# Lending a finished matrix's columns twice as load buffers, and moving mask conversions to earlier column groups

## The chip, the cores and the metric

The kernel runs on one core of a Trainium2 chip. The metric is device time in microseconds, the median of several runs.

## The reference

Two graph layers over N = 4096 nodes with D = 512 features, cut to what matters:

```python
x = layernorm(x + relu(adj @ (step(x) @ sign(w0).T)))        # layer 0
node_att = softmax(x @ node_w, axis=0)                       # layer 1
h = x @ edge_w                                               # <- the stage of this change
e = where(adj > 0, h @ h.T, -9e15)
edge_att = softmax(e, axis=1)
out = adj * (node_att * edge_att) @ (x @ weight) + bias
x = layernorm(x + out)
```

`adj` is 4096 x 4096 in f32, symmetric in where it is not zero, and mostly zero.

## The kernel before, in words

It has three stages, and the middle one is short.

1. Layer 0 (up to 505 us). For each block of 128 rows `adj` is multiplied with the weights. The result is normalised and transposed into `x1T` (feature-major, 4 x 128 features by 4096 nodes).
2. The product with edge_w, `h = x @ edge_w`, kept transposed in `hT` (the same shape: 4 row blocks k = 0 to 3, and 8 columns of 512 nodes, c = 0 to 7). It is what the change touches.
3. `h @ h.T` in blocks, the softmax, and the last product with `adj`.

**The masks.** Stage 3 wants for each pair of nodes a mask that is 0 where there is an edge and a large negative number where there is none. The mask is made ahead of time. A piece of `adj` (128 x 1024, f32, 512 KB) is loaded (`load_mask`, line 411). VectorE turns it, in place, into bf16 (`mask`, line 398, "conversion" from here on). The result (256 KB) is stored to `mask_d` in DRAM (`store`, line 401), and the buffer goes back to the list `bufs`. There are 80 pieces: 54 are made during stage 1, and the last 26 during stage 2.

**Buffers for these 26.** There are four proper ones, named `more`. Eight further ones are parts of `hT` itself: the columns 2, 6, 3 and 7, two row blocks at a time, are empty until the product reaches them. These are the "lent columns". Before the change each of the eight is used once (list `once`): after its store it isn't returned. The other 14 pieces go round on the four `more` buffers.

**The order of stage 2.** The product runs in four column groups g = 0 to 3 ("first" to "fourth"). Group g makes the columns g and g + 4 of `hT`. Each group is one call of `seven`, a scheme that gets a 2 x 2 block product from seven smaller ones (matmuls at line 99); in the second to fourth group three of the seven are split again in the same manner (line 116). The sums are gathered in PSUM banks. ScalarE (ACT) copies from them at lines 163 and 182, and VectorE (DVE) adds from them at lines 184, 191, 172, 166 and 169; a bank can be filled anew once the addition that reads it is done. All three engines work in the order in which the code was written (`manual_schedule`), so an instruction that waits holds up everything behind it on its engine. Lines 137 and 140 are small additions within the split products, line 605 prepares operands on VectorE, and lines 562 to 565 do so on GpSimd (POOL).

**Where the conversions stand.** `seven` calls `between_h` every few matmuls, 48 times in all (`count[0]` = 0 to 47, so twelve per group). At counts chosen by a condition, `between_h` makes one conversion. Three counts later it has ACT issue that piece's store. Then it has SP issue the next load into any buffer that has come free. The loads go through SP's queue and the stores through ACT's, each in order. A load into a used buffer waits for the store that reads it.

**What counts as a conflict.** The layer that places the waits compares, for two accesses to one tile, the stretches from first to last element. Row blocks of `hT` lie one after another, 4096 elements each.

## Time and profile before

| What | Value |
|---|---|
| Median of 3 runs | 1903.18 us (1902.19 to 1904.84) |
| The profiled execution's own time | 1902.74 us |
| Its span in the profile | 1901.0 us |
| Granted TensorE clock | 1.00 in every part of stage 2 |
| Stage 2, first matmul at line 99 to the first at line 885 | 505.31 to 601.29 us |
| Conversions on `more` buffers and in `hT` columns | 18 and 8 |

Busy time by stretch of stage 2 (us within the stretch; the share is that of the 16 DMA engines):

| Stretch, us | PE | DVE | ACT | POOL | DMA share | GB/s |
|---|---|---|---|---|---|---|
| 528 to 552 (second group) | 23.86 | 23.20 | 7.26 | 14.51 | 0.46 | 158 |
| 552 to 575 (third group) | 23.00 | 17.79 | 7.26 | 10.46 | 0.51 | 166 |
| 575 to 601.3 (fourth group) | 24.78 | 18.68 | 8.96 | 1.09 | 0.69 | 226 |

How to read it: PE is TensorE. Its matmuls overlap, and their ends are modelled, so a busy PE isn't one at its best pace; the distance between the starts tells the pace. A note in brackets behind a row of the timeline is the idle time of that engine just before, with the work whose end released it. A row with "x8" is eight instructions of one kind merged.

### The profile page before, as it was taken

The page shows a single profiled execution, that of the slowest core. Times are in us where ns is not written, and L with a number is a line of the kernel's source. Part 1 is how long each engine was busy: PE and PEld are TensorE (multiplying, and loading weights), DVE is VectorE, ACT ScalarE, POOL GpSimd, SP SyncE. Part 2 cuts the span into 40 slices and gives each one's busy share as a digit, 9 for nine tenths or more (in the row PEclk, how much of TensorE's full clock was granted, in tenths as well). Part 3 has the DMA queues.
Part 4 walks back from the last instruction along what each step waited for, and adds up shares of the span by engine and source line. Part 5 has one row for each costly group of instructions (what it writes and reads, how often), then busy time and mean ns, then how long its engine had stood idle before and what let it go on. Part 6 is the DMA issues. An engine that isn't in the chain of part 4 may idle for free.

```text
span 1901.0 us, 21535 instructions
## 1 busy us (share of the span) xinstructions
PE 1888.1 (99%) x7108; PEld 1273.2 (67%) x7108; DVE 1541.7 (81%) x2439; ACT 1039.4 (55%) x1714; POOL 334.9 (18%) x471
## 2 busy tenths in 40 slices
PE   9999999999999999999999999999999999999998
PEld 6888888888655656565567556666666666656646
DVE  7777677777888789788896888898879988898947
ACT  6433333333232567676677667665676567667732
POOL 0133132233550111111120111111111101110100
PEclk9999999999999999999999999999999999999999
DMA  9889898898747478577794978888877877787731
GB/s 324 295 324 359 310 338 322 329 354 291 276 163 262 145 266 341 190 267 274 282 342 165 320 282 294 288 288 297 276 279 285 295 269 281 266 315 251 286 116 56
DMA packets 149936, 521.01 MB, mean 274 GB/s; under 512 B 15040, under 2 KB 21696, under 8 KB 142144
## 3 DMA queue, kind: packets, MB, share of 16 engines
q1 hardware_dynamic: 65392, 235.43, 36.5%
q0 software_dynamic: 65552, 241.72, 33.3%
q10 hardware_dynamic: 18880, 42.47, 6.1%
q8 instruction: 56, 0.92, 0.2%
q14 instruction: 56, 0.46, 0.1%
HBM read 397.93 MB, written 121.63 MB: 273 GB/s over the span
## 4 chain that ended last, share of the span: by engine, by line
PE 87%; DVE 7%; DMA 3%; ACT 2%; issue 1%; SPq 0%; DVEq 0%; ACTq 0%
PE bank L1553 33%; PE acc L525 11%; PE acc L524 11%; PE bank L1151 11%; PE po L1703 4%; PE pt L847 3%; PE bank L946 2%; PE bank L885 2%; PE bank L1110 2%; PE bank L1073 2%; PE seven L99 2%; DVE lent L1322 1%; PE pt L484 1%; DVE slot L1322 1%; PE acc L306 1%
## 5 line engine op out<-in xcount | busy, mean ns | idle before, releaser
L1553 PE MATMUL bank<-lent,lop 128*128 128x256 f32 (+1 forms) x1368 | 433.2, 467 | 1.3 <-DVE lent L1334 0.6
L524 PE MATMUL acc<-xw,hi 128*128 128x512 f32 x960 | 376.5, 392 | 0.0
L525 PE MATMUL acc<-xw,lo 128*128 128x512 f32 x960 | 374.2, 390 | 0.0
L1553 PEld LDWEIGHTS bank<-lent,lop 128*128 128x128 f32 x1368 | 259.2, 190 | 146.7 <-issue 119.6
L1553 PE MATMUL bank<-slot,lop 128*128 128x512 f32 (+1 forms) x928 | 335.5, 508 | 0.7 <-DMA lop<-lop_d 0.5
L1553 PEld LDWEIGHTS bank<-slot,lop 128*128 128x128 f32 x928 | 176.0, 190 | 137.2 <-issue 122.8
L514 ACT CAST hi<-at 128x1024 fp32r<-128x1024 f32 x120 | 126.5, 1054 | 203.2 <-PE acc L524 152.9
L1564 ACT COPY over<-bank 128x512 f32<-128x512 f32 x200 | 116.0, 585 | 195.6 <-PE bank L1553 192.0
L525 PEld LDWEIGHTS acc<-xw,lo 128*128 128x128 f32 x960 | 180.3, 188 | 37.1 <-DVE lo L516 0.3
L524 PEld LDWEIGHTS acc<-xw,hi 128*128 128x128 f32 x960 | 180.3, 188 | 36.8
L516 DVE TENSOR_TENSOR lo<-at,hi 128x1024 fp32r<-128x1024 f32 x120 | 148.9, 1241 | 63.6 <-ACT hi L514 63.2
L818 ACT ACTIVATE line<-line,nmax_c 128x512 f32<-128x512 f32 x160 | 115.4, 727 | 20.9 <-DVE nmax_c L809 20.4
L1715 DVE SCALAR_TENSOR_TENSOR xb<-po,f,xb 128x256 f32<-128x256 f32 x84 | 40.3, 481 | 75.0 <-PE po L1703 74.9
L809 DVE CUSTOM_DVE_ANT_0 line<-lent,slot 128x512 f32<-128x512 bf16 x144 | 93.2, 691 | 8.9 <-ACT slot L848 6.1
L1526 ACT COPY bank<-over 128x512 f32<-128x512 f32 x144 | 86.8, 603 | 0.0
L847 PEld LDWEIGHTS pt<-ident,lent 128*128 128x128 f32 x406 | 50.9, 141 | 36.6 <-issue 23.8
L885 PE MATMUL bank<-hT 128*128 128x512 f32 (+3 forms) x256 | 75.1, 433 | 0.0
L1322 DVE CUSTOM_DVE_ANT_1 lent<-lent,line 128x2048 f32<-128x2048 f32 x32 | 73.0, 2284 | 2.4 <-DMA lent<-s_d 2.4
L485 ACT COPY x1T<-pt 128x512 f32<-128x512 f32 x32 | 18.8, 587 | 101.7 <-PE pt L484 101.7
L848 ACT COPY slot<-pt 128x512 f32<-128x512 f32 (+3 forms) x125 | 68.1, 554 | 11.5 <-PE pt L847 11.5
L1322 DVE CUSTOM_DVE_ANT_1 slot<-slot,line 128x2048 f32<-128x2048 f32 x32 | 73.1, 2284 | 0.0
L1328 ACT ACTIVATE slot<-slot 128x2048 f32<-128x2048 f32 x35 | 67.3, 1924 | 10.2 <-DMA slot<-in_adj_t_dram 10.2
(414 smaller groups left out, 3353.6 us busy)
## 6 DMA issues: line engine op xcount, KB each, us to landing
lop<-lop_d SPq DMA_DIRECT2D x154, 512.0 KB, 4.4
at<-in_adj_t_dram SPq DMA_DIRECT2D x60, 1024.0 KB, 6.9
slot<-in_adj_t_dram POOLq DMA_DIRECT2D x37, 1024.0 KB, 8.0
s_d<-slot POOLq DMA_DIRECT2D x32, 1024.0 KB, 8.1
slot<-s_d POOLq DMA_DIRECT2D x31, 1024.0 KB, 7.4
lent<-s_d POOLq DMA_DIRECT2D x29, 1024.0 KB, 8.0
lent<-in_adj_t_dram POOLq DMA_DIRECT2D x27, 1024.0 KB, 7.8
lent<-in_adj_dram SPq DMA_DIRECT2D x48, 512.0 KB, 6.3
```

The source lines that it names most:

```text
L514: nc.scalar.copy(hi, aq)
L516: nc.vector.tensor_sub(lo, aq, hi.bitcast(F32))
L524: nc.tensor.matmul(acc, hi[:, c, :], xw[:, kb, :], start=(kb == 0), stop=False)
L525: nc.tensor.matmul(acc, lo[:, c, :], xw[:, kb, :], start=False, stop=(kb == NB - 1))
L809: nc.vector.tensor_tensor_reduce(line, mask, src, -1.0, HUGE, ALU.add, ALU.min, accum_out=nmax_c[:, b, c : c + 1])
L818: nc.scalar.activation(line, line, AF.Exp, bias=nmax_c[:, b, c : c + 1], scale=-1.0, accum_out=sum_c[:, b, c : c + 1])
L847: nc.tensor.transpose(pt[:, j, :], src[:, ts(j, P)], ident)
L885: nc.tensor.matmul(pe[:, lo * P :], hT[:, k, ts(A * BG + i, P)], hT[:, k, (B * BG + lo) * P : (B + 1) * W], start=(k == 0), stop=(k == KD ...
L1151: nc.tensor.matmul(ps, left[m][:, k, q, :], right[m][:, k, :], start=(first and k == 0), stop=(k == KD // 2 - 1), skip_group_check=not first,)
L1322: pinned[0](nc.vector._custom_dve(TENSOR_ADD_SAT, out=q, in0=q, in1=m, s0=0.0, s1=-HUGE))
L1553: nc.tensor.matmul(ps, lop[:, k, :], rop[:, k, :], start=start, stop=(k == K - 1), skip_group_check=True)
L1564: nc.scalar.copy(self.to(), self.bank[:, : self.w])
```

## The change

Two things are changed. The lent columns 3 and 7 form a list of their own, `twice`. After its first store such a buffer goes back to `bufs`, so it is loaded a second time, and it is added to `once`, so that the second store is its last. The columns 2 and 6 stay in `once`. In the first round the order of loading is now `more`, columns 3 and 7, columns 2 and 6. Then 10 pieces instead of 14 go round on the `more` buffers.

The condition for the conversions becomes a list of 26 counts. By group (twelve counts each) the conversions were 3, 8, 8 and 7; with the list they are 3, 9, 9 and 5.

```diff
-        once = []
+        once, twice = [], []
...
                 def store():
                     queue.dma_start(mask_d[r][:, c : c + 2, j, :], m)
-                    if not any(a is b for b in once):
-                        bufs.append(a)
+                    for list_ in (once, twice):
+                        if any(a is b for b in list_):
+                            once.append(a)
+                            if list_ is once:
+                                return
+                            break
+                    bufs.append(a)
...
-        once.extend(hT[:, k : k + 2, ts(c, W)] for c in (2, 6, 3, 7) for k in (0, HK))
+        twice, once = ([hT[:, k : k + 2, ts(c, W)] for c in (n, n + HG) for k in (0, HK)] for n in (3, 2))
         bufs.extend(m[:, n, :].rearrange("p (c w) -> p c w", c=2) for m in more for n in range(2))
+        bufs.extend(twice)
         bufs.extend(once)
...
-            if count[0] in (4, 5, 7, 12) or count[0] > 12 and count[0] % 3 and count[0] not in (20,):
+            if count[0] in [4, 5, 7, 12, 13, 14, 16, 17, 18, 19, 21, 22, 24, 25, 26, 28, 29, 30, 32, 33, 34, 36, 37, 39, 41, 42]:
                 if loaded:
                     made.append((count[0], mask(nc.scalar)))
```

Line numbers in the text are those of the kernel before; from line 403 on the changed kernel's lie five or six higher.

## The prediction

> **What bounds the kernel now.** I read the page's first part, then the matmul timeline of the stage that the diff touches, then who keeps it waiting.

> ```profile
> span 1901.0 us, 21535 instructions
> PE 1888.1 (99%) x7108; PEld 1273.2 (67%) x7108; DVE 1541.7 (81%) x2439; ACT 1039.4 (55%) x1714; POOL 334.9 (18%) x471
> ```

> TensorE is the bound throughout; another engine costs time only where it makes TensorE wait. The product with edge_w (lines 99 and 116) runs from 505.31 to 601.29 us, 95.98 us. Its fourth column group ends so (start, duration, instruction, idle before):

> ```profile
> 588.93 3.60 PE L99 MATMUL seven<-x1T,lops 128*128 128x512 f32 x8
> 592.99 3.70 PE L99 MATMUL seven<-t,lops 128*128 128x512 f32 x8 [0.46 <-DVE hT L191]
> 597.75 3.70 PE L99 MATMUL seven<-t,we_s 128*128 128x512 f32 x8 [1.06 <-DVE hT L166]
> 601.29 4.89 PE L885 MATMUL bank<-hT 128*128 128x512 f32 x12
> ```

> Eight such matmuls take 3.43 us from start to start when nothing holds them (569.57 to 573.00 in the third group). Here the three steps take 4.06, 4.76 and 3.54, so 0.63 + 1.33 + 0.11 = 2.07 us are lost. The "idle" at the line's end is less, because the modelled ends overlap. VectorE's timeline says why:

> ```profile
> 588.38 0.69 DVE L398 TENSOR_SCALAR more<-more 128x1024 bf16<-128x1024 f32 x1 [2.63 <-DMA more<-in_adj_dram]
> ...
> 591.65 0.69 DVE L398 TENSOR_SCALAR more<-more 128x1024 bf16<-128x1024 f32 x1
> 592.25 1.28 DVE L191 TENSOR_TENSOR hT<-hT,seven 128x512 f32<-128x512 f32 x2
> 593.45 0.69 DVE L172 TENSOR_TENSOR hT<-hT,seven 128x512 f32<-128x512 f32 x1
> 595.21 0.69 DVE L398 TENSOR_SCALAR more<-more 128x1024 bf16<-128x1024 f32 x1 [1.07 <-DMA more<-in_adj_dram]
> ```

> A mask conversion (L398) waits for its load, and the additions that empty the PSUM banks (L191, L172, L166) queue behind it. The conversions come round on four `more` buffers: store, reload and conversion do not fit between two uses. The second group has a smaller loss of the same kind:

> ```profile
> 542.77 0.69 DVE L398 TENSOR_SCALAR hT<-hT 128x1024 bf16<-128x1024 f32 x1
> ...
> 545.17 0.69 DVE L398 TENSOR_SCALAR hT<-hT 128x1024 bf16<-128x1024 f32 x1
> ...
> 545.89 0.69 DVE L191 TENSOR_TENSOR hT<-hT,seven 128x512 f32<-128x512 f32 x1
> ...
> 546.63 3.70 PE L99 MATMUL seven<-t,lops 128*128 128x512 f32 x8
> ...
> 546.83 0.69 DVE L191 TENSOR_TENSOR hT<-hT,seven 128x512 f32<-128x512 f32 x1 [0.25 <-DMA mask_d<-hT]
> ```

> TensorE starts at 546.63 where 542.89 + 3.43 = 546.32 was possible: it waited for L191, so VectorE has no slack here. The last row is the key one. That L191 writes columns 1 and 5 of hT, yet it waits for the store of a lent buffer in columns 2 or 6. The recorded dependencies cover the whole stretch between a buffer's first and last element: two rows k, k+1 of column c reach over every later column of row k and every earlier one of row k+1. Any two lent buffers with the same two rows thus count as overlapping.

> [...]

> ```profile
> more<-in_adj_dram SPq DMA_DIRECT2D x16, 512.0 KB, 4.8
> mask_d<-more ACTq DMA_DIRECT2D x18, 256.0 KB, 3.5
> hT<-in_adj_dram SPq DMA_DIRECT2D x8, 512.0 KB, 7.7
> mask_d<-hT ACTq DMA_DIRECT2D x8, 256.0 KB, 2.3
> ```

> These are medians, issue to landing, over 500 to 610 us; the shortest load of this line is 3.7 and the shortest store 2.1 us. I go by the trace. [...]

> **The change, part by part.** Number the 26 conversions of this stage 1 to 26. It adds and removes none: 26 conversions at 0.60 us, 26 loads and 26 stores remain, as does every matmul. It moves them: before, 3, 8, 8 and 7 conversions stand in the four groups, after it 3, 9, 9 and 5.

> *Fourth group.* Two conversions fewer, and the last ones take loads issued earlier. Conversion 25 needs the reload that follows the store of conversion 21 (about 576 us): 576 + 2.1 + 4.8 = 583 us, against 585.8 when VectorE comes to it. Conversion 26 likewise: store about 580.8, landing about 588, VectorE there at about 588.3. L191 then starts behind L140 at about 589.6 instead of 592.25, with TensorE needing it only at 592.36. Nothing in the middle holds L166. Gain 2.07 us, say 2.0; if reload 26 takes the 6.7 us of the longest single one here, L137 is 2 us late and still in time.

> *Second group.* Conversions 5 to 8 use the columns 3 and 7 ("twice"), 9 to 12 the columns 2 and 6 ("once"). Positions up to conversion 8 (542.77 to 543.46) are the old ones. Now SP issues four reloads R5 to R8 into columns 3 and 7 right behind the stores of 5 to 8. By the overlap rule R5 also waits for conversion 7, R6 for 8, R7 for 9 and R8 for 10; in turn conversion 9 waits for R5, 10 for R6, 11 for R7 and 12 for R8, though none of these reads that data. Conversions 10, 11 and 12 stand directly ahead of L191, L166 and the second L166.
> - Conversion 9 (new before L137): 0.60 us, and R5 (issued 539.2, landing 543 to 544) hardly holds it.
> - Conversion 10: R6 can't be issued before 543.5. With the shortest landing, 3.7, conversion 10 starts at 547.2, L191 at 547.85 and ends at 548.5, and TensorE starts about 2.0 us later than now. With 4.4 it is 2.6 us, with 4.8 about 3.1, with 6.7 about 5. I take 4.4: the DMA share from 538 to 544 is only 0.33, but from 544 to 550 it is 0.70, with GpSimd's lop_d writes at 542.69 and 543.67. Cost 2.6, bounds 2.0 and 5.
> - Conversion 11: ACT copies L163 first (behind conversion 9, so 544.7 to 545.3), then issues store 7: landing 547.7. R7 lands 4.4 later, 552.1. L166 ends at 552.15 + 0.6 + 0.7 = 553.4; TensorE wants it at 549.25 + 3.43 = 552.7. Cost 0.7, bounds 0 and 2.
> - Conversion 12: store 8 also waits for R6 (they share a semaphore count): 548 + 2.4 + 4.4 = 554.8, so the second L166 ends at 556.2. TensorE, with a half product and four quarters between, wants it at 553.4 + 1.72 + 1.72 = 556.8. Hidden by 0.6 us. On ACT's queue store 10 waits for R8, and the copies L120 queue behind it (about 556 instead of 552.5); TensorE wants them some 4 us into the next group, 557.5. Hidden too, barely.

> SP's queue carries nothing else here: the next stage's loads (from 601.59) wait for the last matmul that reads x1T. Sum for the second group 3.3 us.

> *Third group.* All loads but the late ones are in. Conversion 18 fills an idle 0.94 us that VectorE has at 564.2. One new wait: the first L166 must wait for the store of conversion 18, which ACT issues behind that of 17, which waits for L172 (569.7): 570.2 + 2.1 = 572.3, L166 ends at 573.0, just when TensorE wants it (573.00). With the store at 3.1 it is 1 us late. Cost 0.5, bounds 0 and 2.

> *Afterwards.* The next stage starts behind the last matmul, and TensorE is busy 10.00 of 10 us from 605 to 615; a shift passes on one to one. Sum: 2.6 + 0.7 + 0.5 - 2.0 = +1.8; the bounds of the wait terms lie further above than below, so I take +2.2. The profiled execution took 1902.74 us (span 1901.0); 1902.74 + 2.2 = 1904.9. The median of the runs is 0.44 above it: 1905.4.

> **The rivals.**
> - *New waits outweigh the gain* (forecast): net +0.5 to +3.8, 1905.4; chance 0.50. For it: the chain of L398, reload, L398 is in the built program, and R6 can't be issued earlier.
> - *The waits bite less* (the other side): faster. It decides from the point where R6 lands before VectorE comes to conversion 10 at about 546.0, 2.5 us after issue. Then only conversion 9's 0.60 us is added: 0.6 + 0 + 0.3 - 2.0 = -1.1, 1902.1. Against it: no load here took under 3.7 us. For it: false waits cost only 0.25 us so far, and VectorE might be ahead of the old trace. With the cases that cancel, -2 to +0.5: chance 0.23, of it 0.03 faster by over 0.2%.
> - *The waits pile up*: reloads and stores share the DMA engines and each store waits for a reload, so R6 takes the 7.7 us of the first loads into hT, R7 and R8 follow late, and TensorE waits again at the head of the third group: 6 + 1.5 + 1.5 - 2.0 = +7, 1910; from +3.8 up, chance 0.27. Against it: those eight were queued together at a DMA share of 0.93.

> **How the numbers follow.** 0.2% is 3.8 us, about what a measurement of this kernel can tell from no change. Faster by more 0.03; slower by more 0.27; the rest 0.70. The range leaves out about 0.1 on each side: from 1901.9 (net -1.3) to 1908.9 (net +5.7).

> **What would show it.** In the fourth group L398 with no wait for a load, and steps of 3.43 us up to L885. In the second group, an L398 on hT that waits for a load into hT for 1 to 2 us, directly ahead of L191, and TensorE's step after 542.89 at about 6 us instead of 3.74; a second, smaller one ahead of L166. In the third, L166 waiting for a store of hT. It is wrong if the second group keeps its 23.53 us (528.36 to 551.89, from its first small product to the next group's), or if the fourth still waits for loads.

## The result, and the profile after

| | before | after |
|---|---|---|
| Median of 5 runs, us | 1903.18 (1901.83 to 1904.84) | 1911.77 (1908.17 to 1912.22) |
| Ratio | | 1.0041, 95% interval 1.0026 to 1.0056 |
| The profiled execution's own time, us | 1902.74 | 1911.83 |
| Product with edge_w (first line-99 matmul to the first of the next stage), us | 95.98 | 103.88 |
| Second, third and fourth group, us | 23.53, 22.83, 26.57 | 29.67, 25.49, 25.66 |

The change makes the kernel slower by 0.41%. In the two profiled executions the difference is 9.09 us. Of it 7.90 us lie in the product with edge_w: +6.14 in the second group, +2.66 in the third, -0.91 in the fourth. The product begins 0.30 us earlier, and the rest of the span is 1.49 us longer. That last part is not shown to be the change's: from the end of the product to the end of the span it is 1299.71 us before and 1301.21 here, but 1299.92 in a second profile of the same changed kernel, and over all profiles of this document it lies between 1299.5 and 1301.8 us.

The groups were cut at the first row of their first small product. From line 403 on, line numbers of the changed kernel are five or six higher: L891 is the next stage's first matmul, L416 the load, L611 the operands on VectorE.

The page's head:

```profile
span 1910.1 us, 21532 instructions
PE 1891.0 (99%) x7108; PEld 1275.0 (67%) x7108; DVE 1542.6 (81%) x2439; ACT 1039.9 (54%) x1714; POOL 334.6 (18%) x471
```

TensorE is "busy" for 2.9 us more with the same 7108 matmuls, so idling can't be the whole story: some matmuls became longer. The matmul timeline of the product (start, duration, instruction, idle before):

```profile
542.61 3.60 PE L99 MATMUL seven<-x1T,lops 128*128 128x512 f32 x8
550.78 5.40 PE L99 MATMUL seven<-t,lops 128*128 128x512 f32 x8 [4.58 <-DVE hT L191]
556.02 1.88 PE L99 MATMUL seven<-t,we_s 128*128 128x512 f32 x4
...
575.41 3.60 PE L99 MATMUL seven<-t,lops 128*128 128x512 f32 x8
580.87 2.56 PE L99 MATMUL seven<-t,we_s 128*128 128x512 f32 x4 [1.86 <-DVE hT L166]
...
598.59 3.60 PE L99 MATMUL seven<-x1T,lops 128*128 128x512 f32 x8
602.03 3.60 PE L99 MATMUL seven<-t,lops 128*128 128x512 f32 x8
605.46 3.60 PE L99 MATMUL seven<-t,we_s 128*128 128x512 f32 x8
608.89 3.60 PE L891 MATMUL bank<-hT 128*128 128x512 f32 x8
```

- Fourth group: 3.43 us from each start to the next. The 2.07 us that were lost there are gone.
- Second group: the eight matmuls could start at 542.61 + 3.43 = 546.04 and start at 550.78. That is 4.74 us late, against 0.31 before: +4.43.
- Those eight then take 5.24 us (550.78 to 556.02) instead of 3.54: +1.70, though nothing holds them.
- Third group: 575.41 + 3.43 = 578.84 was possible, 580.87 it is: +2.03.

The windows of the same trace tell why the eight matmuls are slow (columns: stretch, length, busy time of PE, PEld, DVE, ACT and POOL with instructions, granted TensorE clock, DMA share, GB/s):

```profile
550.00:552.00 2.00, 1.22 (x2) 0.53 (x3) 2.00 (x5) 0.00 (x0) 0.00 (x0) 0.85 0.74 229
552.00:554.00 2.00, 2.00 (x4) 0.90 (x3) 0.52 (x1) 0.00 (x0) 0.00 (x0) 0.50 0.74 247
554.00:556.00 2.00, 2.00 (x4) 0.79 (x4) 1.29 (x2) 0.00 (x0) 0.00 (x0) 0.79 0.80 294
...
583.00:585.00 2.00, 2.00 (x6) 1.41 (x5) 1.68 (x4) 0.36 (x1) 0.00 (x0) 0.50 0.34 123
```

The clock is 0.50 shortly behind each of TensorE's two gaps: from 551.41 us, 0.63 us after the matmuls have begun again, and from 582.13 us. Before, it was 1.00 throughout the product. Each of the two stretches is 3413 ns long in the clock records. The second lies across the border of the groups and costs 0.64 us in the third and 1.16 in the fourth. VectorE's timeline shows who made the gaps:

```profile
543.68 0.95 DVE L398 TENSOR_SCALAR hT<-hT 128x1024 bf16<-128x1024 f32 x1 [0.51 <-DMA hT<-in_adj_dram]
...
549.44 0.69 DVE L398 TENSOR_SCALAR hT<-hT 128x1024 bf16<-128x1024 f32 x1 [3.02 <-DMA hT<-in_adj_dram]
550.05 1.28 DVE L191 TENSOR_TENSOR hT<-hT,seven 128x512 f32<-128x512 f32 x2
...
554.20 0.69 DVE L398 TENSOR_SCALAR hT<-hT 128x1024 bf16<-128x1024 f32 x1 [1.68 <-DMA hT<-in_adj_dram]
554.81 0.68 DVE L166 TENSOR_TENSOR hT<-hT,seven 128x512 f32<-128x512 f32 x1
...
580.13 0.69 DVE L166 TENSOR_TENSOR hT<-hT,seven 128x512 f32<-128x512 f32 x1 [2.21 <-DMA mask_d<-hT]
```

Conversions 9, 10 and 11 wait for the reloads R5, R6 and R7, which they don't read, and L191 and L166 queue behind. In the third group L166 waits for a store of a lent buffer. The transfers (500 to 610 us; kind, size, median us from issue to landing):

```profile
hT<-in_adj_dram SPq DMA_DIRECT2D x12, 512.0 KB, 5.9
mask_d<-hT ACTq DMA_DIRECT2D x12, 256.0 KB, 2.7
```

A median hides what decides here. Single transfers of the changed kernel are read by narrow windows. First the issues on ACT and SP (two timelines), then, from the DMA view, the times of store 6 (window 539.3 to 540.2 us) and of R6 (544 to 545.2):

```profile
539.45 0.37 ACTq L401 DMA_DIRECT2D mask_d<-hT  x1
```

```profile
544.40 0.38 SPq L416 DMA_DIRECT2D hT<-in_adj_dram  x1
```

```profile
mask_d<-hT ACTq DMA_DIRECT2D x1, 256.0 KB, 4.9
...
hT<-in_adj_dram SPq DMA_DIRECT2D x1, 512.0 KB, 4.9
```

Store 6 lands at 539.45 + 4.9 = 544.35, and 0.05 us later SP issues R6. In the kernel before the same store, issued at 539.73, took 2.1 us. What is new beside it is R5, whose 512 KB are under way from 538.85 to 543.66; the last experiment but one (e11) tests whether that is the cause.

### The profile page after: what moved, and what is told of

Read it like the earlier page. It is cut to its first block, busy times and chain, and to the rows that moved or that the text cites. A ratio compares the mean times of both kernels' runs of the same rounds, so it can differ in the third digit from the quotient of the medians.

```text
span 1910.1 us, 21532 instructions
## 1 busy us (share of the span) xinstructions
PE 1891.0 (99%) x7108; PEld 1275.0 (67%) x7108; DVE 1542.6 (81%) x2439; ACT 1039.9 (54%) x1714; POOL 334.6 (18%) x471
## 4 chain that ended last, share of the span: by engine, by line
PE 84%; DVE 7%; DMA 4%; issue 3%; ACT 2%; POOL 0%; ACTq 0%; SPq 0%; DVEq 0%; POOLq 0%
PE bank L1559 32%; PE acc L530 11%; PE acc L529 11%; PE bank L1157 9%; PE po L1709 4%; PE seven L99 2%; PE bank L952 2%; PE bank L891 2%; PE pt L853 2%; PE bank L1116 1%; PE bank L1079 1%; DVE lent L1328 1%; DMA lent<-in_adj_dram 1%; PE pt L489 1%; DVE slot L1328 1%
## 5 line engine op out<-in xcount | busy, mean ns | idle before, releaser
L891 PE MATMUL bank<-hT 128*128 128x512 f32 (+3 forms) x256 | 75.1, 433 | 0.0
## 6 DMA issues: line engine op xcount, KB each, us to landing
lop<-lop_d SPq DMA_DIRECT2D x154, 512.0 KB, 4.7
lent<-in_adj_dram SPq DMA_DIRECT2D x48, 512.0 KB, 6.2
```

The lines of the kernel that those rows point to most:

```text
L891: nc.tensor.matmul(pe[:, lo * P :], hT[:, k, ts(A * BG + i, P)], hT[:, k, (B * BG + lo) * P : (B + 1) * W], start=(k == 0), stop=(k == KD ...
```

## The experiments

Each time is the median beside runs of the kernel before on the same chip (1902.5 to 1902.8 us in all four groups of runs).

### Lay hT out column by column

The recorded dependencies compare first to last element: so conversion 10 waited 3.02 us for R6, whose data it doesn't read. With the four row blocks of a column next to each other, a lent buffer is one unbroken stretch, and only real overlaps are left. Besides that, the loads into these columns write rows of 4 KB instead of two of 2 KB. The wrapper that maps the old indices is left out here.

```diff
-        hT = big.tile([P, KD, N], F32, name="hT", tag="large")
+        hT_c = big.tile([P, NG, KD, W], F32, name="hT", tag="large")
+        # hT[p, k, column c] -> hT_c[p, c, k], through a small wrapper
```

With the change (e1):

> The changed kernel with hT laid out column by column, so that each lent buffer is one unbroken stretch; no access, instruction or position is changed, only the recorded overlaps between lent buffers go (and the loads into them write rows of 4 KB instead of two of 2 KB). Theory (waits for overlaps that are none hold VectorE): conversions 10 and 11 no longer wait for reloads, L166 of the third group not for a store; only conversion 9 (0.6 us) stays ahead of L191, the fourth group keeps its gain of 2.1 us, and no half-clock stretch is left: about 1901.7 us (1900.5 to 1903). Rival (the conversions stand too densely, or four more early transfers crowd the DMA engines): the stalls of 4.4 and 2 us stay, 1908 or more.

Measured: 1901.03 us, ratio 0.9992 (0.9984 to 1.0).

```profile
543.03 3.60 PE L99 MATMUL seven<-x1T,lops 128*128 128x512 f32 x8
547.36 3.70 PE L99 MATMUL seven<-t,lops 128*128 128x512 f32 x8 [0.73 <-DVE hT L191]
...
589.65 3.60 PE L99 MATMUL seven<-x1T,lops 128*128 128x512 f32 x8
593.08 3.60 PE L99 MATMUL seven<-t,lops 128*128 128x512 f32 x8
596.52 3.60 PE L99 MATMUL seven<-t,we_s 128*128 128x512 f32 x8
```

The wait ahead of L191 shrinks to 0.90 us (543.03 + 3.43 = 546.46), the one in the third group is gone, the fourth keeps its gain, and the clock stays at 1.00. In the second group the same change, without its false conflicts, loses 0.59 us more at L191 than the kernel before (0.31), which is conversion 9's own time.

Without the change, as a control (e2): the same layout in the kernel before.

> The kernel before with the same layout: the control. Theory: only its one wait of 0.25 us for a store of hT goes, at most 0.3 us: 1902.9 us (1902 to 1904). Rival (the layout itself helps, by longer rows or by access): it gains as much as the changed kernel does from it, 1 us or more.

Measured: 1902.51 us, 0.9999 (0.9991 to 1.0008). So the layout by itself is worth nothing in the kernel before. That kernel has no reloads R5 to R8, so they are looked at in e1 itself: there they take 5.3, 5.5, 6.9 and 4.4 us, against 4.8, 4.9, 4.0 and 4.4 in the changed kernel. The longer rows don't make them land sooner, and e1's 10 us against the changed kernel come from the conflicts that the change adds.

### Half of the change at a time

Buffers alone (e3): `twice` as in the change, the conversions at their old counts.

> The columns used twice, the conversions at the counts of before. Theory: conversions 10, 11 and 12 now stand at counts 22, 23 and 25, behind L191 and the first L166, and R6 has landed by then; L191 waits no more than before, the fourth group has fewer reloads to wait for: 1901.5 to 1904.5 us. Rival (second use of the columns is what costs, wherever the conversions stand): 1908 or more.

Measured: 1909.93 us, 1.0038 (1.0025 to 1.0052). The expectation failed. I had taken conversion 10, at its old count, to lie clear of the reloads. VectorE's timeline:

```profile
549.98 0.69 DVE L191 TENSOR_TENSOR hT<-hT,seven 128x512 f32<-128x512 f32 x1 [3.60 <-DMA mask_d<-hT]
...
559.12 0.69 DVE L398 TENSOR_SCALAR hT<-hT 128x1024 bf16<-128x1024 f32 x1 [6.66 <-DMA hT<-in_adj_dram]
```

The second L191 waits 3.60 us for the store of conversion 7. Conversion 10 stands behind R8 in the program now, and waits 6.66 us for that reload too; L166 queues behind it, and TensorE idles 4.24 us. Lending the columns twice, with overlaps that aren't real, is enough for the loss (the product takes 103.62 us), and where the conversions stand decides which instruction waits.

Counts alone (e4): the kernel before, with the new list of 26 counts.

> The new list of counts, the lent columns used once. Theory: second group as before but for 0.6 us of conversion 9 ahead of L191, no waits for reloads into hT; but 14 pieces go round on four buffers in fewer counts, so L398 waits for loads into more from count 29 on, 2 us or more at a time, and TensorE loses several us in the third and fourth group: 1906 to 1913 us. Rival (the dense counts are what costs in the second group): the 4 us stall stands in the second group here too.

Measured: 1905.36 us, 1.0017 (1.0010 to 1.0024), just under the expected range. TensorE's timeline:

```profile
547.10 3.70 PE L99 MATMUL seven<-t,lops 128*128 128x512 f32 x8 [0.73 <-DVE hT L191]
...
575.98 1.98 PE L99 MATMUL seven<-t,we_s 128*128 128x512 f32 x4 [1.97 <-DVE hT L166]
587.96 1.13 PE L99 MATMUL seven<-x1T,we_s 128*128 128x512 f32 x2 [1.36 <-ACT hT L182]
```

With only the `more` buffers to go round, earlier conversions wait for their loads in the third and fourth group. The second group takes 24.49 us, without the stall of over 4 us, so the dense counts alone don't cause that: the rival falls. Neither half is faster alone: 1.0038 and 1.0017. Neither was tried alone in the layout by columns.

### Lend the other columns first

e5: columns 2 and 6 (used once) go ahead of 3 and 7 (used twice) in the order of loading.

```diff
-        bufs.extend(twice)
         bufs.extend(once)
+        bufs.extend(twice)
```

> The changed kernel, with columns 2 and 6 ahead of 3 and 7 in the order of loading; row blocks of hT lie one after another as before. Theory (false conflicts between lent columns set the waits): the conversions of the second group's middle no longer stand behind reloads that were just issued, since the columns lent once are converted first. The reloads into 3 and 7 now come from the second half of the second group and count as conflicts with the additions into columns 1 and 5 and with the copies and additions of the third group into 2 and 6. So the waits move rather than go: 1908 to 1916 us, with a wait of an L166, L169 or of an L182 copy for a load or store of hT, where TensorE then stands. Rival (what costs is only that conversion 10 stands behind a reload issued too late): with that gone the second group keeps 23.5 to 24.5 us, the gain of the fourth group stays, and the time is 1901 to 1904.

Measured: 1907.19 us, 1.0024 (1.0015 to 1.0032), 0.8 us under the range of the theory and 3 us above the rival's. ACT's timeline, then TensorE's:

```profile
544.80 10.90 ACTq L401 DMA_DIRECT2D mask_d<-hT  x5
555.74 0.63 ACT L120 COPY seven<-own 128x256 f32<-128x256 f32 x2 [10.97 <-PE seven L99]
```

```profile
556.15 0.70 PE L116 MATMUL own<-ends_i,left_i 128*128 128x256 f32 x2 [0.59 <-ACT seven L120]
...
563.90 1.12 PE L99 MATMUL seven<-x1T,we_s 128*128 128x512 f32 x2 [0.51 <-ACT hT L182]
...
577.95 1.98 PE L99 MATMUL seven<-t,we_s 128*128 128x512 f32 x4 [1.18 <-DVE hT L166]
```

L120's 10.97 us are put down to a matmul, but five stores stand ahead of it in ACT's order, and the issue of the last ends at 544.80 + 10.90 = 555.70: ACT waited for what these stores wait for. That last store is issued at 555.34, and a reload into hT landed at 555.26. In the product the clock stays at 1.00 and no gap exceeds 1.4 us. The false waits have moved, as the theory said: the second group is 0.98 us longer than in the kernel before and the third 4.13, in small pieces, while the fourth keeps its gain (24.52 us).

### Keep TensorE from idling

e6: five matmuls whose result nobody reads, ahead of the product that waits for L191, and two at the end of the third group. Each is 0.86 us, two rows of 0.43 in the trace. (The helper `filler` and the counter `turn` are left out here.)

```diff
...
+        filler({2: 5}.get(turn[0], 0))      # second group
         alone(product(1, 6, False, m6))
+        filler({3: 2}.get(turn[0], 0))      # third group
         over[0] = product(1, 3, False, m3)
```

> The changed kernel plus seven matmuls whose result nobody reads (each about 0.86 us): five in the second group between the product that waits for L191 and the next, two at the end of the third group ahead of the product that waits for L166. They fill TensorE's two gaps and take away nothing else. Theory (each gap makes the clock run at half speed for 3.4 us): no half-clock stretch in stage 2, and about 0.5 us back in the second group (there L166 would hold TensorE until about 555.5 anyway) and 1.7 us around the border of the third and fourth: 1909.5 us, ratio about 0.9985 to the changed kernel. Rival (the halving has another cause than TensorE's gap, or the gap need not last long): half-clock stretches stay and the time is that of the changed kernel or up to 2 us longer.

Measured: 1909.21 us, 1.0037 (1.0024 to 1.0049), and no half-clock stretch in the product. The interval overlaps that of the changed kernel, so three kernels were then run on one chip: the changed one (e8), one with only the five fillers of the second group (e9), and both fillers (e10).

> The changed kernel itself once more, beside the two filler kernels on the same chip. Theory (two gaps of TensorE, of about 4.7 and 2.0 us, can each halve its clock for 3.4 us): 1909 to 1912.5 us with a half-clock stretch of 3.4 us behind the first gap at least, and a second group of 29 to 30 us. Rival (the waits of the first profile were an accident of that run): under 1907 us, and the second group under 26 us.

> The changed kernel with only the five matmuls in the second group's gap, none in the third group's. Theory (a gap of 2.0 us alone is enough to halve the clock): no half-clock stretch in the second group, one of 3.4 us at the border of the third and fourth group, costing 1.7 us: 1910.5 to 1911 us. Rival (the second stretch only came because the first gap had thinned out TensorE's work before it, or 2 us is too short): no half-clock stretch in stage 2 at all, and the time of the kernel with both fillers, 1909.2 us.

> The kernel with both fillers once more, so that it stands beside the changed kernel on one chip. Theory: no half-clock stretch in stage 2, and 1.5 to 2.5 us less than the changed kernel in this call (1909.2 us as before). Rival (the stretches cost nothing, since the waits behind them would hold TensorE anyway): the same time as the changed kernel within 0.7 us.

| | median, us | product with edge_w, us | half-clock stretches in it |
|---|---|---|---|
| changed kernel, again (e8) | 1910.65 (1909.25 to 1912.09) | 104.49 | 3, the first two end to end |
| first gap filled (e9) | 1909.85 (1907.71 to 1910.44) | 103.31 | 1 |
| both filled (e10) | 1908.52 (1908.31 to 1912.75) | 101.70 | 0 |

The medians lie in the expected order, though their runs overlap, and e9's lies under its expected range (1910.5 to 1911); the lengths of the product in the profiles are the cleaner reading. Over the two profiles each, the changed kernel's 103.88 and 104.49 stand against 102.13 (e6) and 101.70 (e10): 2.3 us for the stretches, where 2.2 was expected. In e9 the second gap alone halves the clock, so it doesn't need the first:

```profile
580.07 2.69 PE L101 MATMUL seven<-t,we_s 128*128 128x512 f32 x4 [2.22 <-DVE hT L176]
```

(L101 and L176 are the lines 99 and 166 there.) With both filled, TensorE works through the wait and L191's lateness stays:

```profile
546.03 4.46 PE L154 MATMUL filler<-x1T,we_s 128*128 128x512 f32 x10
550.70 3.70 PE L101 MATMUL seven<-t,lops 128*128 128x512 f32 x8 [0.21 <-DVE hT L201]
555.37 1.98 PE L101 MATMUL seven<-t,we_s 128*128 128x512 f32 x4 [0.97 <-DVE hT L176]
```

The last row shows L166's own lateness at full clock: 555.37 - 550.70 - 3.43 = 1.24 us.

### Move one store out of a reload's way

e11: store 6 goes one count earlier, ahead of R5, and R6 keeps its place behind conversion 8.

```diff
-            while made and made[0][0] + 3 <= count[0]:
+            while made and made[0][0] + (2 if made[0][0] == 14 else 3) <= count[0]:
...
-            while bufs and pieces:
+            while len(bufs) > (count[0] == 16) and pieces:
```

> The changed kernel with the store of conversion 6 issued one count earlier, ahead of the reload R5, and R6 kept behind conversion 8 in the program. Theory (the store of conversion 6 takes 4.8 to 5.1 us because R5's load is under way beside it, where it takes 2.1 us without one, and its landing releases R6): that store takes 2.1 to 2.6 us, R6 is issued when conversion 8 ends, about 543.2 us instead of 544.4, and the product that waits for L191 starts 0.8 to 1.3 us earlier, at 549.4 to 550.0 us on the changed kernel's scale, unless the store of conversion 7 holds the second L191. By the overlap rule L182 and L184 of the second group now follow that store and may lose up to 1 us ahead of it, so the whole is 1909.5 to 1911.5 us: the verdict is R6's time behind conversion 8 and not the total. Rival (R6 is late for another cause: SP's queue or conversion 9): it is still issued more than 1 us behind the end of conversion 8, and the store's time doesn't matter.

Measured: 1909.08 us (1906.98 to 1911.44), 1.0034 (1.0020 to 1.0049). The store took 2.4 us. R6 (SP's timeline) follows the end of conversion 8 (542.45 + 0.69) at once:

```profile
543.16 0.38 SPq L416 DMA_DIRECT2D hT<-in_adj_dram  x1
```

It took 4.4 us, and on VectorE and TensorE this followed:

```profile
547.70 0.94 DVE L398 TENSOR_SCALAR hT<-hT 128x1024 bf16<-128x1024 f32 x1 [1.85 <-DMA hT<-in_adj_dram]
```

```profile
539.28 0.67 PE L116 MATMUL own<-right_i,mixed 128*128 128x256 f32 x2 [1.36 <-ACT seven L124]
...
549.29 3.70 PE L99 MATMUL seven<-t,lops 128*128 128x512 f32 x8 [1.60 <-DVE hT L191]
```

L191's product starts at 549.29 instead of 550.78, 1.49 us earlier, more than the 0.8 to 1.3 expected, and by the rival's measure (R6 still over 1 us behind conversion 8) the rival falls. The price was foreseen: L182 now waits for the store, and TensorE loses 1.5 us ahead of it. No stretch of half clock is left in the profiled execution, and its product takes 100.41 us. The median is 0.4 us under the expected range of the whole (1909.5 to 1911.5).

### Move conversion 9 behind L191

e7: e1 with the conversion at count 18 (conversion 9) moved to 20.

> hT laid out column by column with the change, and the conversion at count 18 moved to count 20, so that no additional conversion stands ahead of L137 and L191 in the second group. Theory: the first experiment still lost about 0.7 us in the second group, to the conversion at 18; moved behind L191 it should go: 1900.2 to 1900.8, 0.6 us under the first experiment. Rival (VectorE is as full behind L191, and the conversion at 20 delays L166 or L172 instead): 1901 to 1901.6, the time of the first experiment.

Measured: 1900.59 us, 0.9990 (0.9982 to 0.9998). The second group takes 23.69 us (e1 24.11, before 23.53), and the product 94.09 us, 1.89 less than before. The fourth group's gain is kept whole. The interval lies just under 1; the gain is 0.1%, and that e7 is faster than e1 (1901.03 us) is not shown by the medians, whose runs overlap.

## Why the prediction was wrong, step by step

The forecast named the right mechanism for the waits and the right sign, but put a median of 1905.4 us (1901.9 to 1908.9) where 1911.77 came. On the profiled execution it put +2.2 us and +9.09 came. Two things failed: the stores that release R6 and L166 were given the time of a store that runs alone, and a gap of TensorE was priced at its length, without the clock. The error of 6.9 us falls to these steps:

| Step | Forecast, us | Measured, us |
|---|---|---|
| Conversion 10 and R6, into L191 | 2.6 (2.0 to 5) | 4.43 |
| Conversion 11 and R7, into L166 | 0.7 (0 to 2) | 1.24 at full clock (e10); in the changed kernel it lies under the slow matmuls |
| TensorE at half clock behind the first gap | not in the sum | 1.70 |
| Third group, L166 behind store 18 | 0.5 (0 to 2) | 2.03 |
| TensorE at half clock behind the second gap | not in the sum | 0.64 + 1.16 |
| Fourth group | -2.0 | -2.07 |
| Taken above the sum for the uneven bounds | 0.4 | - |
| Start of the product, and all after it | 0 | -0.30 and +1.49 |

*Fourth group: right,* to 0.1 us, and with the working given. Conversion 9 hardly held by R5: right (0.51 us). It costs nothing in the changed kernel, since conversion 10 waits anyway; it is what e1 loses and e7 gets back.

*R6: the mechanism right, the issue mis-timed.* "R6 can't be issued before 543.5" was worked out from conversion 8 alone. That store 6 would also be in time went unsaid, and it rested on the 2.1 us that this store takes before, when no load runs beside it. The change itself puts R5 there:

| Store 6 | us from issue to landing |
|---|---|
| no R5 beside it: before, e2, e4, e5 | 2.1, 2.5, 2.1, 2.1 |
| moved ahead of R5: e11 | 2.4 |
| R5 issued 0.6 us ahead of it: changed kernel twice, e3, e6, e9, e10 | 4.9, 4.8, 4.9, 4.8, 5.1, 5.1 |
| R5 issued 1.4 us ahead of it: e1, e7 | 4.6, 4.0 |

By these rows a store of ACT's and a load of SP's are not independent: in all eight profiles of the last two rows the 256 KB store lands 0.67 to 0.72 us behind the 512 KB load that was issued ahead of it. The packets of the two interleave only in the last part. The DMA view of the changed kernel, from the store's issue to 541.60 us and from there to its landing (packets, MB, share), has the store's packets on q10 and the load's on q1:

```profile
q1 hardware_dynamic: 163, 0.34, 71.5%
...
q10 hardware_dynamic: 272, 0.26, 27.1%
q1 hardware_dynamic: 116, 0.20, 20.9%
```

The store's first packet moves 2.4 us after its issue, when 192 of the load's 256 have begun (55 to 75% in the eight profiles); in the kernel before it moves 0.9 us after the issue. Why they hold back is not shown. Store 6's late landing made R6's issue 544.40; R6's own time was 4.9 instead of 4.4 us. e11 takes the store away, and R6 is then issued at 543.16 and takes the forecast's 4.4 us. The same slip is in store 7, put at "landing 547.7": issued at 545.33 beside R6 it took 4.7 us and landed at 550.03. The second L191 waits for it, as e3 shows. It ended so close to R6 that curing R6 alone could have gained little; in e11 both came earlier.

*Third group: the same slip.* The store of conversion 18 was given 2.1 us, at most 3.1. It took 4.0, beside two loads into `more` issued at 572.7 and 573.9 and two more stores; the DMA share from 576 to 579 us was 0.98. That these slowed it is argued from the trace; no run moved this store alone. The issue itself came as forecast: 570.2 plus the 5.85 by which the third group starts later is 576.05, and 576.01 was measured.

*The clock: missing.* A wait of TensorE was priced at its length. The rows behind the two gaps show a second price: 1.70 and 1.80 us. Without it L166 would have held TensorE 1.3 us behind the first, so taking both away gives 2.3 us (e6, e10 against the changed kernel), not 3.5.

*The rivals.* "The waits pile up" came nearest in time (1910 us), but in part by luck, for another reason than it gave: it put 6 us on the second group through a reload of 7.7 us, and what came was 4.4 us of wait and 1.7 of clock. It named TensorE's wait at the head of the third group, and none is there. L120 and the second L166, both called hidden, were hidden. "The waits bite less" fell, as no load came quickly enough.

## What to carry to other kernels

When a change issues new transfers, price every store and load that now runs beside them, not by its time when alone (store 6: 2.1 us alone, 4.9 beside R5); the one that waits for the slowed store is where it is paid. Lend a buffer out of a larger tile only in a form in which its first-to-last stretch holds nothing else: here that layout alone turned 1.0041 into 0.9992. And where a change opens a gap on TensorE of about 2 us or more (the shortest that was followed by half clock here is 2.03), put a stretch at half clock (1.7 us here) into the upper bound: whether it is paid depends on where the gap falls, as the next section shows.

## What was unexpected of the hardware

In the product each stretch at half clock is 3413 ns long (in e8 the first is 6827, two end to end), and some come behind gaps that are much shorter than that. A gap is the actual start less the earliest possible one. The length of a gap alone doesn't decide:

| TensorE's gap, us | Idle in the window of 3413 ns that holds most of it, us | Half clock in the next window |
|---|---|---|
| 4.74 and 4.43 (changed kernel, twice), 4.41 (e3) | 2.78, 2.49, 3.41 | yes, all |
| 2.57 (e3, ahead of its second L191's product) | 1.66 | no |
| 2.03, 2.14, 2.38 (third group: changed kernel twice, e9) | 1.86, 1.98, 2.22 | yes, all |
| 2.13 (third group, e4) | 1.59 | no |
| 1.77, 1.78 (e11) | 1.10, 1.46 | no |
| 1.33 and less (before) | 1.06 at most | no |

The middle column follows from the clock records. In each profile all changes of the clock are whole multiples of 3413.3 ns apart (in the changed kernel 160, 1, 8, 1 and 387 of them). So the changes lie on a grid of windows, whose position differs from execution to execution: a border is at 551.41 us of the span in the changed kernel and at 550.08 us in e3. Continued from its changes through the changed kernel (first four rows) and e3 (last two), the grid gives these windows (columns as above; idle is the length less PE's busy time):

```profile
544.59:548.00 3.41, 1.61 (x4) 0.38 (x2) 1.83 (x4) 0.59 (x1) 1.42 (x3) 1.00 0.91 250
548.00:551.41 3.41, 0.63 (x2) 0.39 (x3) 1.97 (x4) 0.00 (x0) 1.38 (x2) 1.00 0.61 195
551.41:554.83 3.42, 3.42 (x6) 1.36 (x5) 1.74 (x4) 0.00 (x0) 0.00 (x0) 0.50 0.76 267
578.72:582.13 3.41, 1.55 (x4) 0.68 (x4) 2.00 (x4) 0.00 (x0) 0.00 (x0) 1.00 0.20 69
...
546.67:550.08 3.41, 1.75 (x4) 0.44 (x3) 0.10 (x1) 0.00 (x0) 1.66 (x3) 1.00 0.66 212
550.08:553.49 3.41, 2.77 (x7) 1.17 (x8) 2.38 (x4) 0.00 (x0) 0.00 (x0) 1.00 0.62 165
```

So the same gap can be paid in one execution and not in the next. The runs of e9 fit: four have a mean clock of 0.998 and take 1909.71 to 1910.44 us, and two have 1.000, which leaves no room for such a stretch, and take 1907.71 and 1908.79. No run moved a gap within its window on purpose.
